# Inverse roots of the norms: from a power on GpSimd to Newton steps on VectorE, with shorter gaps between the steps of a chain

## The chip, the cores and the metric

The kernel runs on one core of a Trainium2 chip. The time is device microseconds of one execution, given as the median of several runs; a smaller number is better. A profile of one execution of the kernel before stands beside the times. In the profile PE is TensorE's matmuls and PEld its weight loads, DVE is VectorE, ACT is ScalarE, POOL is GpSimd and SP is SyncE, from which most DMAs are issued.

## The reference

Two transformer layers, each an attention part and a mixture of experts, are applied to 8 sequences of 256 tokens with 128 features. Each of the four parts takes a layer norm of its input and adds its result to the residual:

```python
def _layernorm(x, axis=-1, eps=1e-05):
    m = jnp.mean(x, axis=axis, keepdims=True)
    v = jnp.var(x, axis=axis, keepdims=True)
    return (x - m) / jnp.sqrt(v + eps)

x = x + _L0_attn_ref(_layernorm(x), ...)   # latent-projection attention, 16 heads, causal softmax
x = x + _L0_ffn_ref(_layernorm(x), ...)    # top 2 of 8 experts, gelu; the result is normed again
x = x + _L1_attn_ref(_layernorm(x), ...)   # RMS norm, linear attention in segments of 32
x = x + _L1_ffn_ref(_layernorm(x), ...)    # top 2 of 8 experts, relu
```

Layer 0's expert part ends in a norm of its own, `(out - mean) * rsqrt(var + 1e-5) * gamma + beta`. Layer 1's attention takes an RMS norm of the layer-normed input. In both expert parts a router picks two of eight experts for each token. All is in fp32.

## The kernel before, in words

The 2048 tokens are worked on as four blocks of 512 (`NBLK` = 4; a block is four tiles of 128 tokens). Layer 0's attention goes by rows, one row being one sequence, so two rows make a block and there are eight in all (`Row`, `attention0`). A row's norm is of two tiles (values 128x2), a block's of four (128x4).

After attention a block goes through the router (`route0` or `route1`: norm, logits, top 2), `dispatch` (each token gets slots, and POOL scatters the rows `hrows` to DRAM with 8 indirect DMAs), `experts` (15 tiles of slots, each with weights loaded by SP; ACT applies the function to the hidden layer at L510), `chosen` (POOL gathers the two results `yt` of each token with 8 indirect DMAs) and then `combine0` and `before1` (layer 0: weigh and norm the results, then norms, projections and gates for layer 1's attention) or `finish` (layer 1: add and store).

The order of the work is written out by hand. Steps are Python generators. `beside` runs the steps of attention, and after each of them `Lines.go` advances a clock of its own: PART0 is 2.0 units in 4 slots, PART1 is 1.5 units in 3 slots, so a slot is half a unit. In each slot at most one step of the line "chain" (routers, dispatches, gathers, combines) is put down, and experts by credit. A chain step is due again `APART` = 1.0 unit after it ran, or after what it yields:

```python
wait = next(steps, self)
if wait is not self:
    if line == "chain":
        queue.append((self.now + (wait or APART), steps, then))
```

What is put down in this way is ordered by a scheduler of the language into one list for each engine; `behind(...)` and `follow(...)` tie instructions to a place in it. Each engine then works through its list in order, and an instruction at the head of a list that waits for another engine holds up everything behind it.

There are 24 norms: eight of rows, four in `route0`, four in `combine0`, four in `before1` and four in `route1`. In 20 of them `rsqrt` (L272) adds the epsilon on DVE (L275), has POOL raise to the power -0.5 with the constant tile `mhalf` (L276), and DVE scales with the result (L295 in `layernorm`, L930 in `combine0`). In `before1` the layer norm and the RMS norm are made together: four small DVE instructions (L945 to L948), one power of 128x8 on POOL (L950), and the scaling at L955. In the routers and in the rows the scaling is put off by one step (`later[0]()`), after a gap of 1.5 units in the routers, as after the power in `combine0` and `before1`; a row's steps follow those of attention.

Of the kernel before, what the change touches and what calls it, by code (L numbers as in the profile page):

```python
# [36 lines left out]
ALU = mybir.AluOpType  # L37
# [3 lines left out]
P = 128  # L41
B, S, D = 8, 256, 128
NBLK = 4
NT = 4
# [34 lines left out]
def two_layers(  # L79
# [6 lines left out]
    nc = tc.nc  # L86
    cp = ctx.enter_context(tc.tile_pool(name="const", bufs=1))
    wk = ctx.enter_context(tc.tile_pool(name="work", bufs=2))
    sm = ctx.enter_context(tc.tile_pool(name="small", bufs=3))
# [8 lines left out]
    def tl(pool, shape, tag, dt=FP, bufs=None):  # L98
        kw = {} if bufs is None else {"bufs": bufs}
        return pool.tile(shape, dt, tag=tag, name=f"{tag}_{next(names)}", **kw)  # L100

    def bank():
        return tl(ps1, [P, 512], "mm")
# [16 lines left out]
    @contextmanager  # L120
    def behind(*engines):

        seen = reversed(nc.cur_bb.bb.instructions)
        want, found = set(engines), []
        for i in seen:
            if i.engine in want:
                want.remove(i.engine)
                found.append(i)
                if not want:
                    break  # L130
        with ExitStack() as stack:
            for i in found:
                stack.enter_context(tc.issue_after(i))
            yield
# [58 lines left out]

    ident = tl(cp, [P, P], "ident")
    make_identity(nc, ident)
    mhalf = tl(cp, [P, 2 * NT], "mhalf")
    nc.gpsimd.memset(mhalf, -0.5)
    wqkv = tl(cp, [P, QK + KVH * HD], "wqkv")
    identb = tl(cp, [P, P], "identb", BF)
    causb, within = tl(cp, [P, G, P], "causb", BF), tl(cp, [P, G, 32], "within", BF)  # L200
# [67 lines left out]

    def rsqrt(src, eps):

        n = src.shape[1]
        r = tl(sm, [P, NT], "rsqrt")[:, 0:n]
        nc.vector.tensor_scalar(r, src, eps, None, ALU.add)  # L275
        nc.gpsimd.tensor_tensor(r, r, mhalf[:, 0:n], ALU.pow)  # L276
        return r

    def moments(src):
        n = src.shape[1]  # L280
# [7 lines left out]
    def layernorm(src, y, parts=None):  # L288

        mv = moments(src)  # L290
        r = rsqrt(mv[:, :, 1], 1e-5)

        def scaled():
            for t in range(src.shape[1]):
                nc.vector.tensor_scalar(  # L295
                    y[:, t, :], src[:, t, :], mv[:, t, 0:1], r[:, t : t + 1],
                    ALU.subtract, ALU.mult,
                )

        if parts is None:  # L300
            scaled()
        else:
            parts.append(scaled)
        return y

    def transposed(src, tag, eng, bufs=2):

        n = src.shape[1]
        pt = bank()
        for t in range(n):  # L310
            nc.tensor.transpose(pt[:, t * P : (t + 1) * P], src[:, t, :], ident)
        y = tl(wk, [P, n * P], tag, bufs=bufs)
        (nc.scalar.copy if eng == "act" else nc.vector.tensor_copy)(y, pt[:, 0 : n * P])
        return y

    def per_tile(ap):

        return ap.unsqueeze(1).to_broadcast([P, NT, ap.shape[1]])

    def last(ap, n):  # L320

        return ap.unsqueeze(2).to_broadcast([P, ap.shape[1], n])

    def small(tag, shape=(P, NT, E)):
        return tl(sm, list(shape), tag)
# [32 lines left out]
    def logits(xT, gw):  # L358
        pg = bank()
        for t in range(NT):  # L360
            nc.tensor.matmul(
                pg[:, t * E : (t + 1) * E], lhsT=xT[:, t * P : (t + 1) * P], rhs=gw,
                start=True, stop=True,
            )
        return pg[:, 0 : NT * E].rearrange("p (t e) -> p t e", e=E)
# [202 lines left out]
    def gated_bias(gates, b2s):  # L568

        pg = bank()  # L570
        for t in range(NT):
            nc.tensor.transpose(pg[0:E, t * P : (t + 1) * P], gates[:, t, :], ident)
        gT = tl(wk, [E, BT], "qm")
        nc.scalar.copy(gT, pg[0:E, :])
        pb = bank()
        for t in range(NT):
            nc.tensor.matmul(
                pb[:, t * P : (t + 1) * P], lhsT=gT[:, t * P : (t + 1) * P], rhs=b2s,
                start=True, stop=True,
            )  # L580
        return pb.rearrange("p (t o) -> p t o", t=NT)
# [287 lines left out]
    def route0(x, half):  # L869
        later = []  # L870
        xn = layernorm(x, half.rows, later)
        yield 1.5 * APART
        later[0]()
        nc.gpsimd.tensor_tensor(x, x, per_tile(bet), ALU.add)
        yield
        with behind(PE):
            xT = transposed(xn, "xTf", "vec")
        yield
        lg = small("lg")
        with behind(PE):  # L880
            nc.vector.tensor_copy(lg, logits(xT, gw0))
            psh = bank().rearrange("p (t o) -> p t o", t=NT)
            for t in range(NT):
                nc.tensor.matmul(
                    psh[:, t, :], lhsT=xT[:, t * P : (t + 1) * P], rhs=shw, start=True, stop=True
                )
        half.acc = acc = tl(wk, [P, NT, D], "acc", bufs=NBLK)
        nc.vector.tensor_tensor(acc, psh, per_tile(shb), ALU.add)
        hots = half.hots
        m1, m2 = top2(lg, hots)  # L890
        yield 2 * APART
        yield from dispatch(half, b1s0)
        tot = small("tot", (P, NT))
        nc.vector.tensor_tensor(tot, m1, m2, ALU.add)
        nc.vector.reciprocal(tot, tot)
        gates = tl(wk, [P, 2, NT, E], "gates")
        for k, m in enumerate((m1, m2)):
            g = half.gates[:, k, :]
            nc.vector.tensor_tensor(g, m, tot, ALU.mult)
            nc.vector.tensor_tensor(gates[:, k], hots[:, k], last(g, E), ALU.mult)  # L900
        nc.vector.tensor_tensor(gates[:, 0], gates[:, 0], gates[:, 1], ALU.add)
        nc.scalar.activation(acc, acc, AF.Gelu)
        yield
        with behind(PE):
            nc.vector.scalar_tensor_tensor(
                acc, acc, 0.5, gated_bias(gates[:, 0], b2s0), ALU.mult, ALU.add
            )

    def combine0(x, half, yt):
        acc = half.acc  # L910
        with behind(DVE):
            for t in range(NT):
                for k in range(2):
                    nc.vector.scalar_tensor_tensor(
                        acc[:, t, :], yt[:, k, t, :], half.gates[:, k, t : t + 1],
                        acc[:, t, :], ALU.mult, ALU.add,
                    )
        yield

        with behind(DVE):  # L920
            mv = moments(acc)
            r = rsqrt(mv[:, :, 1], 1e-5)
            for t in range(NT):
                nc.vector.scalar_tensor_tensor(
                    acc[:, t, :], acc[:, t, :], mv[:, t, 0:1], gam, ALU.subtract, ALU.mult
                )
        yield 1.5 * APART
        with behind(DVE):
            for t in range(NT):
                nc.vector.scalar_tensor_tensor(  # L930
                    x[:, t, :], acc[:, t, :], r[:, t : t + 1], x[:, t, :], ALU.mult, ALU.add
                )
# [5 lines left out]
    def before1(o, x):  # L938
# [3 lines left out]
        with behind(DVE):  # L942
            mv = moments(x)
            v, rr = mv[:, :, 1], small("norms", (P, 2, NT))
            nc.vector.tensor_scalar(rr[:, 0], v, 1e-5, None, ALU.add)  # L945
            nc.vector.reciprocal(rr[:, 1], rr[:, 0])
            nc.vector.tensor_tensor(rr[:, 1], rr[:, 1], v, ALU.mult)
            nc.vector.tensor_scalar(rr[:, 1], rr[:, 1], 1e-6, None, ALU.add)  # L948
            rr = rr.rearrange("p a t -> p (a t)")
            nc.gpsimd.tensor_tensor(rr, rr, mhalf, ALU.pow)  # L950
        r = rr[:, NT:]
        yield 1.5 * APART
        with behind(DVE):
            for t in range(NT):
                nc.vector.tensor_scalar(  # L955
# [284 lines left out]
    def route1(x, half):  # L1240
        later = []
        xn = layernorm(x, half.rows, later)
        yield 1.5 * APART
        later[0]()
        yield
        with behind(PE):
            xT = transposed(xn, "xTf", "vec")
        yield
        lg, hots = small("lg"), half.hots
        with behind(PE):  # L1250
            nc.vector.tensor_tensor(lg, logits(xT, gw1), per_tile(gb1), ALU.add)
        top2(lg, hots)
        yield 2 * APART
        yield from dispatch(half, b1s1)
        gates = tl(wk, [P, NT, E], "gates")
        nc.vector.tensor_tensor(gates, hots[:, 0], hots[:, 1], ALU.add)
        yield
        with behind(PE):
            nc.vector.tensor_tensor(x, gated_bias(gates, b2s1), x, ALU.add)
# [46 lines left out]
    APART = 1.0  # L1306
# [163 lines left out]
```

## Time and profile before

| | |
|---|---|
| median of 3 runs | 710.58 us (708.97 to 712.07) |
| profiled execution | 705.73 us, span 704.0 us |
| granted TensorE clock, mean | 0.912 of full speed |
| busy: PE, DVE, ACT, POOL | 569.2, 406.4, 333.9, 190.0 us |
| the powers on POOL | 20 of 927 ns and 4 of 1807 ns |

Busy time is the sum of an engine's instructions. A group of instructions is shown as line, engine, operation, output and inputs with their shapes and count, then its busy time and the mean ns of one, then the engine's idle time just before them with what ended it. In the table of waits, each row names who waited, for whom, the total in us, how often, and the longest. In the timeline, each row has the start, the duration, and in brackets the idle time before it. In the page's second part a digit is the busy share in one of 40 equal slices of the span.

### The profile page before, as it was taken

To read this page: it belongs to the slowest core of one execution; us is meant where nothing else is said; L and a number is where in the kernel's file an instruction comes from. 1 tells how busy PE (TensorE), PEld (TensorE's weight loads), DVE (VectorE), ACT (ScalarE), POOL (GpSimd) and SP (SyncE) were. 2 spreads that over 40 slices of the span, in tenths; PEclk is the share of its full clock that TensorE was granted. 3 is DMA by queue.
4 is the path that set the end of the run, shared out by engine and by line. 5 is a ranking of instruction groups with operands and counts; after the bars stand their busy time and mean duration, and the time that the engine had idled before them with its cause. 6 is when DMAs were issued, how large, how long until landed. Compare 5 with 4: busy or idle time off the path is not lost. (4 is left out here: it accounts for less than half of the span.)

```text
span 704.0 us, 13677 instructions
## 1 busy us (share of the span) xinstructions
PE 569.2 (81%) x4830; PEld 427.4 (61%) x4846; DVE 406.4 (58%) x1193; ACT 333.9 (47%) x761; POOL 190.0 (27%) x223
## 2 busy tenths in 40 slices
PE   5577786998989788967899579979889898988570
PEld 3233353676646466536688467758867788987570
DVE  4765665536645566536687289787875877531201
ACT  2233342877858489842464224633444233443240
POOL 4201105001144210442113511434603340441204
PEclk9999988999899899997999779989998999999795
DMA  6800004453164414453345624546464658878662
GB/s 163 225 2 0 1 2 138 132 169 114 35 187 132 119 47 135 132 150 95 97 125 170 209 62 139 159 124 172 136 198 138 183 162 239 248 228 272 170 180 56
DMA packets 132100, 95.81 MB, mean 136 GB/s; under 512 B 8817, under 2 KB 114369, under 8 KB 132033
## 3 DMA queue, kind: packets, MB, share of 16 engines
q1 hardware_dynamic: 127520, 85.58, 41.7%
q0 software_dynamic: 4096, 8.40, 4.2%
q10 hardware_dynamic: 416, 0.96, 0.5%
q8 instruction: 39, 0.64, 0.4%
q14 instruction: 29, 0.23, 0.1%
HBM read 77.87 MB, written 17.04 MB: 135 GB/s over the span
## 5 line engine op out<-in xcount | busy, mean ns | idle before, releaser
L510 ACT ACTIVATE hT<-mm,bias 128x128 f32<-128x128 f32 x480 | 136.3, 371 | 136.3 <-PE mm L503 127.8
L503 PE MATMUL mm<-xrT,w 128*128 128x128 f32 x960 | 140.7, 295 | 23.9 <-DMA w<-in_w 10.4
L503 PEld LDWEIGHTS mm<-xrT,w 128*128 128x128 f32 x960 | 126.5, 206 | 41.4 <-DVE xrT L487 12.6
L515 PE MATMUL mm<-w,hT 128*128 128x128 f32 x960 | 137.4, 285 | 7.5 <-ACT hT L510 5.3
L515 PEld LDWEIGHTS mm<-w,hT 128*128 128x128 f32 x960 | 123.4, 198 | 17.7 <-ACT hT L510 13.7
L432 POOL DMA_INDIRECT xg<-hrows,slots x64 | 66.0, 1032 | 110.3 <-DVE slots L424 56.0
L559 POOL DMA_INDIRECT yt<-yg,slots x64 | 61.3, 958 | 110.3 <-issue 50.0
L727 ACT ACTIVATE at<-sc 128x1024 f32<-128x1024 f32 x48 | 48.8, 1023 | 56.3 <-PE sc L780 56.1
L780 PE MATMUL sc<-qm,kxT 32*128 32x512 f32 x192 | 54.9, 682 | 11.5 <-ACT at L727 4.6
L780 PE MATMUL sc<-km,qT 32*128 32x512 f32 x192 | 55.6, 701 | 4.2 <-DVE qx L688 2.3
L688 DVE TENSOR_REDUCE nmax<-sc 128x8 f32<-128x1024 f32 x32 | 38.9, 1220 | 24.9 <-PE sc L780 24.9
L276 POOL TENSOR_TENSOR rsqrt<-rsqrt,mhalf 128x4 f32<-128x4 f32 (+1 forms) x20 | 18.5, 927 | 122.7 <-DVE rsqrt L275 98.1
L523 DVE COPY ys<-mm 128x512 f32<-128x512 f32 (+1 forms) x32 | 20.8, 651 | 38.7 <-PE mm L515 38.5
L1120 DVE TENSOR_TENSOR at<-sc,consts 128x1024 f32<-128x1024 f32 x32 | 38.0, 1214 | 6.2 <-PE sc L1115 5.8
L510 ACT ACT_TABLE_LOAD x25 | 32.1, 1283 | 15.3 <-PE mm L503 15.0
L780 PEld LDWEIGHTS <-identb 32*32 32x32 bf16 (+1 forms) x320 | 7.6, 91 | 39.2 <-issue 37.3
L1058 POOL TENSOR_TENSOR vm<-va,consts 128x432 f32<-128x432 f32 x16 | 14.6, 932 | 59.2 <-ACT hT L510 19.7
L487 DVE COPY xrT<-mm 128x512 f32<-128x512 f32 (+1 forms) x32 | 20.8, 651 | 15.9 <-PE mm L486 15.8
L738 PE MATMUL mm<-at,vx 128*32 128x512 f32 x192 | 26.7, 630 | 4.1 <-ACT at L727 4.0
L780 PEld LDWEIGHTS sc<-qm,kxT 32*128 32x128 f32 x192 | 14.4, 191 | 25.0 <-issue 9.4
L1115 PE MATMUL sc<-pqm,kT 32*128 32x512 f32 x128 | 23.2, 800 | 6.9 <-DVE at L1120 4.9
L1139 ACT COPY rope<-mm 128x512 f32<-128x512 f32 x16 | 9.4, 588 | 40.3 <-PE mm L1133 40.3
(212 smaller groups left out, 935.6 us busy)
## 6 DMA issues: line engine op xcount, KB each, us to landing
w<-in_w SPq DMA_DIRECT2D x240, 256.0 KB, 3.4
xr<-xg SPq DMA_DIRECT2D x24, 256.0 KB, 3.2
yg<-ys SPq DMA_DIRECT2D x24, 256.0 KB, 4.5
xg<-zero SPq DMA_DIRECT2D x12, 256.0 KB, 2.9
xr<-xg SPq DMA_DIRECT2D x8, 192.0 KB, 5.2
yg<-ys SPq DMA_DIRECT2D x8, 192.0 KB, 4.1
x<-in_x SPq DMA_DIRECT2D x4, 256.0 KB
xg<-hrows,slots POOLq DMA_INDIRECT x64, 2.2
```

The lines of the kernel that those rows point to most:

```text
L432: i = nc.gpsimd.indirect_dma_start(out=xg_h[:, :], out_offset=bass.IndirectOffsetOnAxis(ap=half.slots[:, k, t : t + 1], axis=0), in_=half. ...
L487: nc.vector.tensor_copy(xrT[:, 0 : n * P], pt[:, 0 : n * P])
L503: nc.tensor.matmul(ph[:, c * P : (c + 1) * P], lhsT=w1s[:, c * P : (c + 1) * P], rhs=xrT[:, t * P : (t + 1) * P], start=True, stop=True,)
L510: nc.scalar.activation(hT[:, c, :], src, func, bias=bias)
L515: nc.tensor.matmul(po[:, t * D : (t + 1) * D], lhsT=hT[:, c, :], rhs=w2s[:, c, :], start=(c == 0), stop=(c == NC - 1),)
L559: nc.gpsimd.indirect_dma_start(out=yt[:, k, t, :], out_offset=None, in_=yg[half.h][:, :], in_offset=bass.IndirectOffsetOnAxis(ap=half.slot ...
L688: return nc.vector.tensor_reduce(nm[:, js[0] : js[0] + 2, :], sc.rearrange("p j (i k) -> p j i k", i=G), AX.X, ALU.max, negate=True,)
L727: return nc.scalar.activation(pT[:, js[0] : js[0] + 2, :], sc, AF.Exp)
L738: nc.tensor.matmul(self.po[32 * j : 32 * j + 32, :], lhsT=self.vx[:, kt, j, :], rhs=self.pT_of[s][:, j, :], start=(kt == 0), stop=(kt == qt),)
L780: done[n].append(nc.tensor.matmul(*args, **kw))
L1115: nc.tensor.matmul(sc[j].rearrange("p (i k) -> p i k", i=G), lhsT=pkT[rows, cols], rhs=pqm[rows, :, cols], start=True, stop=True,)
L1120: nc.vector.tensor_tensor(at[:, 2 * a : 2 * a + 2].rearrange("p j i k -> p (j i) k"), d.rearrange("p j (i k) -> p (j i) k", i=G), const("t ...
```

## The change

The inverse root is worked out on DVE. A first guess comes from the bits of the value: they are shifted right by one as an integer, negated, and a constant is added. Then three Newton steps of three instructions each are taken, so a root is 11 instructions on 128x2, 128x4 or 128x8 values, each of which reads what the one before wrote. POOL no longer takes part, and the constant tile `mhalf` goes. In `route0`, `combine0`, `before1` and `route1` the gap of 1.5 units behind the norm's statistics becomes the usual 1.0, which is two slots where it was three. The rows of layer 0's attention have no such gap.

```diff
-    mhalf = tl(cp, [P, 2 * NT], "mhalf")
-    nc.gpsimd.memset(mhalf, -0.5)
...
+    def root(v):
+
+        n = v.shape[1]
+        y, z = (tl(sm, [P, 2 * NT], k, bufs=4)[:, 0:n] for k in ("root", "step"))
+        yi = tl(sm, [P, 2 * NT], "rooti", I32)[:, 0:n]
+        nc.vector.tensor_scalar(yi, v.bitcast(I32), 1, None, ALU.logical_shift_right)
+        nc.vector.tensor_scalar(y.bitcast(I32), yi, -1.0, float(0x5F3759DF), ALU.mult, ALU.add)
+        for _ in range(3):
+            nc.vector.tensor_tensor(z, v, y, ALU.mult)
+            nc.vector.scalar_tensor_tensor(z, z, -0.5, y, ALU.mult, ALU.mult)
+            nc.vector.scalar_tensor_tensor(y, z, 1.5, y, ALU.add, ALU.mult)
+        return y
+
     def rsqrt(src, eps):
 
-        n = src.shape[1]
-        r = tl(sm, [P, NT], "rsqrt")[:, 0:n]
-        nc.vector.tensor_scalar(r, src, eps, None, ALU.add)
-        nc.gpsimd.tensor_tensor(r, r, mhalf[:, 0:n], ALU.pow)
-        return r
+        v = tl(sm, [P, NT], "rsqrt")[:, 0 : src.shape[1]]
+        nc.vector.tensor_scalar(v, src, eps, None, ALU.add)
+        return root(v)
...
     # route0, combine0, before1 and route1, once each
-        yield 1.5 * APART
+        yield
...
     # before1
-            rr = rr.rearrange("p a t -> p (a t)")
-            nc.gpsimd.tensor_tensor(rr, rr, mhalf, ALU.pow)
+            rr = root(rr.rearrange("p a t -> p (a t)"))
```

More of the change, by code (lines that the diff above doesn't have):

```diff
@@ L266, in values_of_zeros @@
             nc.gpsimd.memset(by_head(t)[:, :, :, HD], 1.0)
-    def rsqrt(src, eps):
-        n = src.shape[1]
-        r = tl(sm, [P, NT], "rsqrt")[:, 0:n]
-        nc.vector.tensor_scalar(r, src, eps, None, ALU.add)
-        nc.gpsimd.tensor_tensor(r, r, mhalf[:, 0:n], ALU.pow)
-        return r
+    I32 = mybir.dt.int32
+    def root(v):
[9 more added lines that the diff above has]
+        return y
+    def rsqrt(src, eps):
+        v = tl(sm, [P, NT], "rsqrt")[:, 0 : src.shape[1]]
+        nc.vector.tensor_scalar(v, src, eps, None, ALU.add)
+        return root(v)
     def moments(src):
@@ L926, in combine0 @@
                 )
-        yield 1.5 * APART
+        yield
         with behind(DVE):
@@ L948, in before1 @@
             nc.vector.tensor_scalar(rr[:, 1], rr[:, 1], 1e-6, None, ALU.add)
-            rr = rr.rearrange("p a t -> p (a t)")
-            nc.gpsimd.tensor_tensor(rr, rr, mhalf, ALU.pow)
+            rr = root(rr.rearrange("p a t -> p (a t)"))
         r = rr[:, NT:]
-        yield 1.5 * APART
+        yield
         with behind(DVE):
@@ L1242, in route1 @@
         xn = layernorm(x, half.rows, later)
-        yield 1.5 * APART
+        yield
         later[0]()
```

## The prediction

> **What bounds the kernel now.** I read the page first, then the groups by line (idle before each group), the table of waits, and the timeline where the waits are long.
>
> ```profile
> span 704.0 us, 13677 instructions
> PE 569.2 (81%) x4830; PEld 427.4 (61%) x4846; DVE 406.4 (58%) x1193; ACT 333.9 (47%) x761; POOL 190.0 (27%) x223
> DVE  4765665536645566536687289787875877531201
> ```
>
> TensorE (PE) is busy 81% of the span, and its order is fixed[...]. VectorE (DVE) has 58% on average, but in the middle of the second half single slices stand at 8 and 9 tenths. GpSimd (POOL) has time to spare; what matters there is its queue.
>
> ```profile
> L276 POOL TENSOR_TENSOR rsqrt<-rsqrt,mhalf 128x4 f32<-128x4 f32 (+1 forms) x20 | 18.5, 927 | 122.7 <-DVE rsqrt L275 98.1 <-DVE mv L285 24.4
> L950 POOL TENSOR_TENSOR norms<-norms,mhalf 128x8 f32<-128x8 f32 x4 | 7.2, 1807 | 27.6 <-DVE norms L948 16.7 <-DVE mv L285 10.9
> L295 DVE TENSOR_SCALAR hrows<-x,mv,rsqrt 128x128 f32<-128x128 f32 x32 | 9.1, 342 | 21.6 <-POOL rsqrt L276 21.6
> L295 DVE TENSOR_SCALAR xn<-x,mv,rsqrt 128x128 f32<-128x128 f32 x16 | 5.0, 340 | 14.1 <-POOL rsqrt L276 14.1
> L930 DVE SCALAR_TENSOR_TENSOR x<-acc,rsqrt,x 128x128 f32<-128x128 f32 x16 | 4.8, 346 | 3.8 <-POOL rsqrt L276 3.8
> L955 DVE TENSOR_SCALAR xl<-x,mv,norms 128x128 f32<-128x128 f32 x16 | 4.4, 340 | 2.5 <-POOL norms L950 2.5
> ```
>
> There are 24 norms (20 + 4). A power takes POOL 0.93 or 1.81 us, and DVE stands still for its result 21.6 + 14.1 + 3.8 + 2.5 = 42.0 us in all. Four of these waits are far longer than a power: 13.43, 6.79, 4.61 and 2.83 us, 27.7 together; in those the power stood on POOL's queue behind eight (the last: four) indirect DMAs of about 1.25 us. The other 14.3 us are about 0.8 a norm. What the long ones cost PE is in the waits and in the timeline around 404 us:
>
> ```profile
> PE mm L311 <- DVE xrT L487: 9.9, 1, 9.9
> PE mm L587 <- DVE on L760: 7.9, 3, 6.1
> ```
>
> ```profile
> 400.50 0.94 POOL L559 DMA_INDIRECT yt<-yg,slots  x1 [0.30 <-issue]
> 401.46 1.78 POOL L1058 TENSOR_TENSOR vm<-va,consts 128x432 f32<-128x432 f32 x2
> 403.19 1.05 POOL L276 TENSOR_TENSOR rsqrt<-rsqrt,mhalf 128x4 f32<-128x4 f32 x1
> ```
>
> ```profile
> 390.67 0.17 DVE L275 TENSOR_SCALAR rsqrt<-mv 128x4 f32<-128x4 f32 x1
> 404.27 1.11 DVE L295 TENSOR_SCALAR hrows<-x,mv,rsqrt 128x128 f32<-128x128 f32 x4 [13.43 <-POOL rsqrt L276]
> 408.16 2.18 DVE L914 SCALAR_TENSOR_TENSOR acc<-yt,hgates,acc 128x128 f32<-128x128 f32 x8
> ```
>
> PE lost 9.9 us in the 13.43 us stall, 6.1 (the longest of L587) in the 6.79, 1.3 in the 4.61 and nothing in the 2.83: 17.3 of 27.7.
>
> **The change, part by part.**
>
> *1. Price of a root on DVE.* Eleven instructions on 128x2 to 128x8, each reading the one before. The nearest rows are a chain of small DVE instructions in the router:
>
> ```profile
> 608.56 0.18 DVE L335 RECIPROCAL ssum<-ssum 128x4 f32<-128x4 f32 x1
> 608.77 0.19 DVE L336 TENSOR_TENSOR sm<-sm,ssum 128x32 f32<-128x32 f32 x1
> 609.00 0.19 DVE L346 TENSOR_REDUCE top<-sm 128x4 f32<-128x32 f32 x1
> ```
>
> So 0.21 to 0.23 us from start to start when each waits for the last; 0.21 for these smaller shapes, 2.3 us a root. The integer shift and the integer multiply-add have no row; between 0.15 (a plain 128x4 scalar op) and twice that each, I take the plain one; the upper end adds 24 x 2 x 0.15 = 7 us of DVE. An independent instruction starts only about 0.1 us after the one before, so a step with other work ahead of it adds some 0.1. In the built order of the changed kernel, 179 of the 240 steps inside roots follow their predecessor directly and 61 have something between. Added DVE time: (24 + 179) x 0.21 + 61 x 0.1 = 49 us against 42 us of stalls removed. For DVE as a whole it is nearly an exchange; the places decide.
>
> [...]
>
> *2. The start: +5.5.* In the changed order DVE does row 0's root, row 1's statistics, row 1's root, and only then the copy that PE waits for.
>
> ```profile
> 4.54 0.17 DVE L275 TENSOR_SCALAR rsqrt<-mv 128x2 f32<-128x2 f32 x1
> 5.43 0.27 DVE L213 COPY oT<-mm 64x128 f32<-64x128 f32 x1
> 5.75 0.79 PE L214 MATMUL mm<-wqb,oT 64*128 64x128 f32 x2 [1.12 <-DVE oT L213]
> ```
>
> The copy at 5.43 moves to 4.75 + 2.3 + 1.3 (statistics and two scalings, as now) + 2.3 + 0.3 = about 10.9. PE's chain to the first scores hangs on it and no other work covers it.
>
> *3. The long stalls: -13.* The power leaves POOL's queue, so the DMAs no longer stand ahead of it. At 404 us the next thing late is the gather itself: in the changed order the eight L914 (there L925) still stand ahead of the copy that the router's matmuls need, and the last gathered rows land at about 403, so that copy moves from 410.3 to some 404: -6 of PE's 9.9. At 119 us the operand that PE lacked now stands ahead of the scaling: -6. Of the other two, -1.
>
> *4. The other 18 norms: +11.* Their share of the added DVE time is 49 - 4.6 (start) - 7.5 (the four above) = 37; less 14.3 of old stalls, +22.5 us. On DVE's queue the score maxima (L688), the masks on scores (L1120) or the scalings stand directly behind, and PE waits for those. The long stalls gave PE 17.3/27.7 = 0.6 of their length; short ones meet more slack, so I take 0.5. Bounds: 0 (all in slack) and 0.8.
>
> *5. Activation tables: +2.5.* The build has 61 table loads where there were 57; a row gives 1.28 us each, 5.1 on ScalarE, between PE's hidden layer and its outputs. Half is taken, 0 and 5 are the ends.
>
> *6. The shorter gaps: 0.* Four steps a block come half a unit of the line's time earlier. The moved steps issue no DMA, but dispatch scatters, gathers, their stores and weight loads follow them in the queues of POOL and SP. In the built order PE is the same up to about 230 us; behind that the dispatch positions of the second layer stand 29 and 19 matmuls earlier, 36 later and unchanged, out of the program's 2774, and the last block's rows and all after it stand where they were. The gather in front of the 308 to 330 us gap (PE lost 7.8 there) stands as before. No direction follows; the ends are -8 and +10, one gap of that kind closed or opened. POOL's freed 26 us and the dropped memset cost nothing: POOL is 27% busy.
>
> Sum: 5.5 - 13 + 11 + 2.5 + 0 = +6 us. The profiled execution took 705.73 us (span 704.0 and 1.7 around it), so 711.7 in its terms; it stands 0.7% under the median, 710.58, and on that the forecast is 716.6.
>
> **The rivals.** *Faster: DVE's queue has slack where the roots go.* If the roots of step 4 fall into time in which DVE would wait for PE anyway (the table of waits has 24.9 us of L688's `nmax` waiting for scores), and the long stalls return all 17.3 us, the sum is 5.5 - 17.3 + 0.15 x 22.5 + 2.5 = -6: 704.6. It decides from the point where PE sees less than about a quarter of the short places. For it: DVE at 58%. Against it: slices at 8 and 9 tenths, and roots directly ahead of L688.
>
> *Slower by more: DVE becomes the bound between 420 and 570 us.* There it is busy 17 to 19 of 22 us. At a share of 0.8, with a new gap like that at 308 us: 5.5 - 13 + 18 + 2.5 + 3 = +16: 726.6. Against it: 21 us of stalls leave the same stretch.
>
> *No change.* Start, short places and long stalls cancel: 710.6.
>
> **How the numbers follow.** About 0.5%, 3.6 us, is what a measurement of this kernel can tell from no change. Likeliest case 0.56 (716.6, own range 711 to 723, from shares 0.3 to 0.75), faster 0.17, far slower 0.15, no change 0.12. With the likeliest case's lower edge counted as no change: faster 0.17, same 0.20, slower 0.63. The range 703 to 729 reaches into both outer cases.
>
> **What would show it.** Right: eleven roots' steps at 0.2 us pitch; L214 starting near 11 us; no DVE wait on POOL at a scaling; the 9.9 us PE wait shrunk to about 4 and the 6.1 gone; DVE busy up by some 40 us; more waits of PE for DVE on scores. Wrong: a pitch near 0.1, a start that moves by under 3 us, PE waits on L688 and L1120 unchanged, or one new gap of PE above 8 us, which would make step 6 the main term.

## The result and the profile after

| | before | after |
|---|---|---|
| median | 705.39 us (701.88 to 712.07, 20 runs) | 713.56 us (709.28 to 722.05, 20 runs) |
| profiled execution | 705.73 us, span 704.0 | 716.5 us, span 714.7 |
| granted TensorE clock, mean | 0.912 | 0.909 |

The changed kernel takes 1.0106 of the time before, with a 95% interval of 1.0074 to 1.0137. That is 7.5 us on the median before (5.2 to 9.7). The medians themselves stand 8.2 us apart, the two profiled executions 10.8. (Here and below, ratios and intervals are of the fast executions alone, those within 1.5% of their kernel's fastest, while medians are of all executions, so the two can differ.)

The page of the changed kernel, its span, the busy row, and VectorE in 40 slices:

```profile
span 714.7 us, 13929 instructions
PE 574.0 (80%) x4830; PEld 431.2 (60%) x4846; DVE 443.5 (62%) x1457; ACT 339.3 (47%) x765; POOL 165.1 (23%) x198
DVE  5665578446575755724687869786988787531111
```

DVE has 264 more instructions (24 roots of 11) and 37 us more of busy time. POOL has lost 25 us. PE is busy 4.8 us more for the same 4830 matmuls, and its idle time (span less busy time) has grown from 134.8 to 140.7 us, by 5.9. So in this pair of profiles the loss is of two kinds: longer waits of PE, and matmuls that took longer. The second kind differs from execution to execution (see the last section). The groups by line show what one step of a root costs (busy us in all and mean ns of one stand behind the bar):

```profile
L280 DVE SCALAR_TENSOR_TENSOR step<-step,root 128x4 f32<-128x4 f32 (+2 forms) x72 | 12.4, 173 | 1.6
L281 DVE SCALAR_TENSOR_TENSOR root<-step,root 128x4 f32<-128x4 f32 (+2 forms) x72 | 11.3, 158 | 1.6
L279 DVE TENSOR_TENSOR step<-rsqrt,root 128x4 f32<-128x4 f32 (+1 forms) x60 | 9.6, 160 | 1.4
```

Nothing on DVE waits for POOL at a scaling any more: L306, the scaling that was L295, had 21.6 + 14.1 us of it and now has no such wait. What PE waits for has changed its kind. The table of waits, PE's longest rows and those on scores (total us, times, longest):

```profile
PE mm L514 <- DVE xrT L498: 13.9, 7, 3.9
PE mm L322 <- DVE xl L965: 11.3, 4, 7.1
PE mm L763 <- DVE os L755: 7.6, 1, 7.6
PE sc L791 <- DVE qx L699: 6.8, 4, 2.7
PE mm L514 <- DMA w<-in_w: 6.6, 3, 3.8
PE mm L212 <- DMA x<-in_x: 6.6, 1, 6.6
...
PE mm L322 <- DVE hrows L306: 4.5, 2, 2.5
...
PE sc L791 <- DVE nmax L699: 4.3, 3, 1.8
...
PE sc L1125 <- DVE at L1130: 0.3, 1, 0.3
```

The waits on scores before (maxima at L688, masks at L1120):

```profile
PE sc L1115 <- DVE at L1120: 4.9, 2, 3.9
PE sc L780 <- DVE nmax L688: 4.8, 3, 2.1
...
PE sc L780 <- DVE qx L688: 4.5, 4, 2.3
```

The single 9.9 us wait and the 6.1 us wait of before are gone. In their place stand a 6.6 us wait in the first matmuls (put down to the load of `x`, though what came last is DVE's copy, as the next view shows), more waits for the copies of transposed rows (L498), and somewhat longer ones for the score maxima: L699 (before L688), 11.1 us in all where they were 9.3. The waits for the masks fell from 4.9 to 0.3.

The start, in DVE's timeline of the changed kernel:

```profile
4.32 0.17 DVE L287 TENSOR_SCALAR rsqrt<-mv 128x2 f32<-128x2 f32 x1
4.53 0.17 DVE L276 TENSOR_SCALAR rooti<-rsqrt 128x2 int32<-128x2 int32 x1
4.73 0.17 DVE L277 TENSOR_SCALAR root<-rooti 128x2 int32<-128x2 int32 x1
4.93 0.16 DVE L279 TENSOR_TENSOR step<-rsqrt,root 128x2 f32<-128x2 f32 x1
...
6.50 0.16 DVE L281 SCALAR_TENSOR_TENSOR root<-step,root 128x2 f32<-128x2 f32 x1
...
7.61 0.16 DVE L287 TENSOR_SCALAR rsqrt<-mv 128x2 f32<-128x2 f32 x1
...
10.70 0.27 DVE L211 COPY oT<-mm 64x128 f32<-64x128 f32 x1
```

and in PE's:

```profile
11.03 0.79 PE L212 MATMUL mm<-wqb,oT 64*128 64x128 f32 x2 [6.56 <-DMA x<-in_x]
```

A step follows the last after 0.20 us (ten steps in 1.97 us, from 4.53 to 6.50). Two roots stand ahead of the copy at 10.70, and the matmul that needs it starts at 11.03, where it started at 5.75 before: +5.3 us.

A row's norm in the middle of layer 0, DVE's timeline:

```profile
60.90 0.17 DVE L287 TENSOR_SCALAR rsqrt<-mv 128x2 f32<-128x2 f32 x1
61.11 0.17 DVE L276 TENSOR_SCALAR rooti<-rsqrt 128x2 int32<-128x2 int32 x1
...
63.28 0.60 DVE L306 TENSOR_SCALAR xn<-x,mv,root 128x128 f32<-128x128 f32 x2
63.80 1.22 DVE L699 TENSOR_REDUCE qx<-sc 128x8 f32<-128x1024 f32 x1
```

and PE's:

```profile
65.16 0.74 PE L791 MATMUL sc<-qm,kxT 32*128 32x512 f32 x2 [2.69 <-DVE qx L699]
```

The score maximum, 1.22 us of DVE, waits behind the root, and PE's next scores wait for that maximum: 2.69 us with nothing else to do. It is one of the places that the loss comes from; what it costs is measured below, in rows_on_pool.

The former 404 us stall, first PE and then DVE:

```profile
417.98 1.00 PE L322 MATMUL mm<-ident,hrows 128*128 128x128 f32 x4 [2.52 <-DVE hrows L306]
...
425.28 1.16 PE L514 MATMUL mm<-xrT,w 128*128 128x128 f32 x8 [2.21 <-DVE xTf L324]
```

```profile
417.22 0.35 DVE L925 SCALAR_TENSOR_TENSOR acc<-yt,hgates,acc 128x128 f32<-128x128 f32 x1 [4.20 <-DMA yt<-yg,slots]
417.49 1.11 DVE L306 TENSOR_SCALAR hrows<-x,mv,root 128x128 f32<-128x128 f32 x4
```

PE waits 2.5 + 2.2 us where it waited 9.9. DVE stood 4.20 us for gathered rows just ahead of the scaling: the power is no longer late, the gather is. In DVE's order two of the eight instructions that take gathered rows (L925) stand ahead of the scaling, so the scaling still comes 10.2 us after its add of epsilon (407.34 to 417.49), where the power made it 13.6.

The former 119 us stall, PE's timeline, now later in the same chain:

```profile
137.05 1.08 PE L497 MATMUL mm<-ident,xr 128*128 128x128 f32 x4 [4.25 <-DMA xr<-xg]
```

PE's 6.1 us wait is gone, and shortly after that place PE waits 4.25 us for the load of scattered rows.

### The profile page after: what moved, and what is told of

It reads as the page before. It is cut to its first block, busy times and chain, and to the rows that moved or that the text cites. A ratio compares the mean times of both kernels' runs of the same rounds, so it can differ in the third digit from the quotient of the medians.

```text
span 714.7 us, 13929 instructions
## 1 busy us (share of the span) xinstructions
PE 574.0 (80%) x4830; PEld 431.2 (60%) x4846; DVE 443.5 (62%) x1457; ACT 339.3 (47%) x765; POOL 165.1 (23%) x198
## 5 line engine op out<-in xcount | busy, mean ns | idle before, releaser
L514 PE MATMUL mm<-xrT,w 128*128 128x128 f32 x960 | 144.5, 301 | 26.4 <-DVE xrT L498 13.9
L514 PEld LDWEIGHTS mm<-xrT,w 128*128 128x128 f32 x960 | 130.9, 213 | 41.1 <-DVE xrT L498 16.7
L791 PE MATMUL sc<-qm,kxT 32*128 32x512 f32 x192 | 57.0, 706 | 12.0 <-DVE qx L699 5.1
L791 PE MATMUL sc<-km,qT 32*128 32x512 f32 x192 | 58.1, 731 | 3.6 <-DVE nmax L699 1.8
L699 DVE TENSOR_REDUCE nmax<-sc 128x8 f32<-128x1024 f32 x32 | 38.9, 1221 | 22.9 <-PE sc L791 22.9
L498 DVE COPY xrT<-mm 128x512 f32<-128x512 f32 (+1 forms) x32 | 20.8, 652 | 23.6 <-PE mm L497 23.6
L699 DVE TENSOR_REDUCE qx<-sc 128x8 f32<-128x1024 f32 x16 | 19.6, 1223 | 13.5 <-PE sc L791 13.3
L633 POOL TENSOR_TENSOR x<-x,bout 128x256 f32<-128x256 f32 x8 | 5.8, 723 | 80.8 <-DVE xn L306 47.3
```

The source lines that it names most:

```text
L498: nc.vector.tensor_copy(xrT[:, 0 : n * P], pt[:, 0 : n * P])
L514: nc.tensor.matmul(ph[:, c * P : (c + 1) * P], lhsT=w1s[:, c * P : (c + 1) * P], rhs=xrT[:, t * P : (t + 1) * P], start=True, stop=True,)
L699: return nc.vector.tensor_reduce(nm[:, js[0] : js[0] + 2, :], sc.rearrange("p j (i k) -> p j i k", i=G), AX.X, ALU.max, negate=True,)
L791: done[n].append(nc.tensor.matmul(*args, **kw))
```

## The experiments

The twelve kernels ran in three groups, each on another chip. The first and third chip granted TensorE a mean clock of 0.86 to 0.88 in the profiles (the kernel before takes 754 to 755 us there), the second one near 0.91 (707 us). So every ratio below is to the kernel before in the same group, and ratios of different groups are set side by side only with that in mind. Each ratio is of five rounds, with its 95% interval.

Norms are told apart as "rows" (the eight norms of layer 0's attention, on 128x2 values) and "blocks" (the other sixteen).

### Group 1: roots and gaps apart (before: 754.34 us)

**roots_only**, the roots without the shorter gaps:

```diff
     # route0, combine0, before1 and route1 of the changed kernel
-        yield
+        yield 1.5 * APART
```

> The roots on VectorE, the gaps of 1.5 units kept: TensorE's order is that of the kernel before but for a few rows. Theory (the roots' own time on VectorE, at places where TensorE waits for it): all of the loss is here, +8 us against the kernel before (ratio 1.011, 1.007 to 1.015), with the first scores 5.3 us later as in the changed kernel. Rival 1 (the moved chain steps, that is the new order, cost the time): ratio 1.000 to 1.004. Rival 2 (the two parts are worth as much each): 1.005.

Measured: 762.76 us, 1.0122 [1.0070, 1.0173]. The roots alone carry the whole loss, within this interval.

**gaps_only**, the shorter gaps with the powers still on POOL:

```diff
     # route0, combine0, before1 and route1 of the kernel before
-        yield 1.5 * APART
+        yield
```

> The power on GpSimd as before, the four gaps at 1.0 unit: TensorE's order is nearly that of the changed kernel. Theory (the roots' own time): no change beyond 2 us either way, ratio 0.997 to 1.003. Rival 1 (the order): +6 to +8 us, ratio 1.009 to 1.011. Rival 2 (half each): 1.005.

Measured: 752.06 us, 0.9937 [0.9903, 0.9970]; ACT has 765 instructions, as in the changed kernel, where the kernel before has 761. So the four extra activation-table loads (61 after, 57 before, 1.28 us each) come with the gaps, not with the roots, and the gaps cost nothing in spite of them. DVE still waits for the powers (before, the same two rows had 21.6 us with 13.4 as the longest, and 14.1 with 6.8):

```profile
DVE hrows L295 <- POOL rsqrt L276: 16.4, 6, 10.0
...
DVE xn L295 <- POOL rsqrt L276: 13.9, 7, 6.8
```

What exactly the gaps gain was not found, and its size is not secured: the medians of all executions, 752.06 and 754.34 us, stand 0.3% apart. With the roots in place the gaps returned about 0.1% (1.0122 against 1.0106, on different chips and inside both intervals). Whether the two parts add is not resolved.

**start_on_pool**, the changed kernel with the norms of the first two rows by a power on POOL:

```diff
     def rsqrt(src, eps):
...
         nc.vector.tensor_scalar(v, src, eps, None, ALU.add)
-        return root(v)
+        norms_made.append(src.shape[1])
+        if len(norms_made) <= 2:
+            nc.gpsimd.tensor_tensor(v, v, mhalf[:, 0 : src.shape[1]], ALU.pow)
+            return v
+        return root(v)
```

> The changed kernel, but the norms of the first two rows are raised to the power on GpSimd; everything else is as in the changed kernel. Theory (a delay at the start is passed on to the end): 5.3 us less than the changed kernel, so +3 us against the kernel before, ratio 1.004. Rival (later waits for loads and gathers swallow the early delay): no less than the changed kernel, ratio 1.011.

Measured: 762.81 us, 1.0101 [1.0041, 1.0160]. At 124 us it lags the kernel before by 7.8 us, where roots_only lags by 13.2, so the 5.4 us of the start are there; at the end the interval cannot tell it from the changed kernel, and the theory's 1.004 lies just outside it. That the start's loss reaches the end is not shown by this run (rows_on_pool, below, does show it in PE's waits).

**six_steps**, six Newton steps for three:

```diff
-        for _ in range(3):
+        for _ in range(6):
```

> The changed kernel with six Newton steps where it has three: each root has 9 more instructions at 0.197 us, 1.8 us more on VectorE in each of the 24 norms, 42 us of VectorE time in all. Theory (TensorE sees the whole root at the start and about half of it elsewhere): 3.6 us more at the start and 20 elsewhere, about +32 us against the kernel before, ratio 1.045. Rival (VectorE has slack at all places but the start): +12 us, ratio 1.017.

Measured: 800.48 us, 1.0626 [1.0574, 1.0678]. 24 x 9 more instructions at 0.197 us are 42.6 us of DVE; against the changed kernel's 1.0112 (after_again, on another chip) the time grew by 0.051 of 754 us, about 39 us. Against start_on_pool, on the same chip, PE's idle time in the profile grew by 29 us (152.2 to 181.5). The waits of PE show where:

```profile
PE mm L322 <- DVE xl L965: 29.8, 4, 11.9
PE mm L514 <- DVE xrT L498: 11.9, 5, 4.5
PE sc L791 <- DVE nmax L699: 10.8, 4, 6.4
```

The wait for the four block scalings of L965 is 29.8 us, against 11.3 in the changed kernel (13.5 in start_on_pool, on the same chip) and 8.6 in gaps_only, which has the short gaps and the powers. So the roots of 2.2 us add 3 to 5 us there, and the further 1.8 us in each of the four add 16 or more.

### Group 2: which norms (before: 706.96 us)

**after_again** is the changed kernel once more, with no edit, to have it on the same chip as the next three.

> The changed kernel once more, on the chip on which its variants run, as their mark. Ratio to the kernel before 1.011 (1.007 to 1.014). If the parts add up, the roots alone (1.0122) and the gaps alone (0.9937) would give 1.006; if they do not, 1.011.

Measured: 715.54 us, 1.0112 [1.0049, 1.0175].

**two_steps**, the same line with `range(2)`; the root is less exact, its last step left out:

```diff
-        for _ in range(3):
+        for _ in range(2):
```

> The changed kernel with two Newton steps instead of three (the roots are less exact): 3 instructions fewer in each of 24 roots, 14.2 us of VectorE time at 0.197 us each. Theory A (VectorE time added inside a root shows nearly in full, as six steps did: 39 us more than the changed kernel for 42 us): 13 us less than the changed kernel, ratio to before about 0.993. Theory B (half of it shows, as the prediction took): 7 us less, ratio 1.001.

Measured: 705.57 us, 0.9959 [0.9932, 0.9987]. 72 instructions, 14.2 us of DVE, are worth 0.0153 x 707 = 10.8 us: a share of 0.76. The interval of after_again alone is 4.5 us to each side, so this run by itself does not exclude the 0.5 that the prediction took for most norms. PE's idle time in the two profiles, 140.2 us in after_again and 128.7 here, agrees with the larger share (its profiled execution took 711.1 us, more than the median), and so do the 39 of 42.6 us of the longer root. Together they say that DVE's root is on PE's path for most of its length, all norms taken together.

**rows_on_pool**, the changed kernel with the power on POOL in the eight rows' norms; the sixteen block norms keep their roots:

```diff
+        if src.shape[1] == 2:
+            nc.gpsimd.tensor_tensor(v, v, mhalf[:, 0 : src.shape[1]], ALU.pow)
+            return v
         return root(v)
```

> The changed kernel, but the eight norms of rows raise to the power on GpSimd; the 16 norms of blocks keep the root on VectorE. TensorE's order is that of the changed kernel. Theory A (the full time shows): the start gains 5.3 us, four rows 1.4 us each, and the two long waits of rows come back with 6.7 us net: 4 us less than the changed kernel, ratio to before 1.005. Theory B (only the start and the long waits show): 1.4 us more than the changed kernel, ratio 1.013.

Measured: 701.41 us, 0.9919 [0.9892, 0.9947]. Every theory missed, and by much: 0.0193, or 13.6 us, less than the changed kernel, with the order of PE's matmuls the same. The place shown above, in DVE's timeline of this kernel:

```profile
56.59 0.17 DVE L294 TENSOR_SCALAR rsqrt<-mv 128x2 f32<-128x2 f32 x1
57.58 0.60 DVE L317 TENSOR_SCALAR xn<-x,mv,rsqrt 128x128 f32<-128x128 f32 x2 [0.82 <-POOL rsqrt L297]
58.10 1.22 DVE L710 TENSOR_REDUCE qx<-sc 128x8 f32<-128x1024 f32 x1
```

and PE's:

```profile
59.46 0.70 PE L802 MATMUL sc<-qm,kxT 32*128 32x512 f32 x2 [1.29 <-DVE qx L710]
```

From the add of epsilon to the maximum it takes 1.51 us (56.59 to 58.10) where the root makes it 2.90 (60.90 to 63.80): 1.4 us, and PE's wait shows just that, 2.69 against 1.29. All waits for the maxima together are 7.2 us here and 11.4 in after_again. As the order of the matmuls is the same, the lead over after_again at any matmul splits into idle time and busy time of PE up to it (us, at the time of after_again):

| at | 25 | 75 | 125 | 200 | 225 | 300 | 400 | 500 | 600 |
|---|---|---|---|---|---|---|---|---|---|
| lead | 5.5 | 7.8 | 8.7 | 8.6 | 5.3 | 11.9 | 12.0 | 11.9 | 9.7 |
| of it less waiting | 5.5 | 7.7 | 8.7 | 9.0 | 8.4 | 9.2 | 9.5 | 9.5 | 9.0 |
| of it shorter matmuls | 0.0 | 0.1 | 0.0 | -0.5 | -3.0 | 2.6 | 2.5 | 2.4 | 0.7 |

So the rows' roots cost PE some 9 us of waits, 5.5 at the start and 3.5 at the other six, and these are kept: they stand between 8.4 and 9.5 at all later points of the table, and over the whole span they are 12.5 (140.2 against 127.7). What comes and goes is the matmuls' own time. The profiled executions differ by 10.1 us at the end, the medians by 14.1; the interval on 13.6 is near 5 us to each side.

**long_stalls_only**: short gaps, powers on POOL in 21 norms, and the root on DVE only in the three norms whose power had stood longest behind POOL's DMAs (the sixth and the eighth row's, and the first block's router norm of layer 1):

```diff
+        if len(norms_made) - 1 not in (6, 9, 14):
+            nc.gpsimd.tensor_tensor(v, v, mhalf[:, 0 : src.shape[1]], ALU.pow)
+            return v
         return root(v)
...
     # before1
-            rr = root(rr.rearrange("p a t -> p (a t)"))
+            rr = rr.rearrange("p a t -> p (a t)")
+            nc.gpsimd.tensor_tensor(rr, rr, mhalf, ALU.pow)
```

> The short gaps, the power on GpSimd in 21 norms, and the root on VectorE only in the three where the power stood behind eight indirect DMAs (waits of 6.8, 4.3 and 10.0 us in the profile of the gaps alone). TensorE's order is exactly that of the gaps alone. Theory A (a stall of VectorE shows nearly in full): 21.1 us of waits against 6.6 us of roots, 14 us less than the gaps alone, ratio to before 0.975. Theory B (behind the stall the next instruction waits for the gathered rows anyway): 2 to 6 us less than the gaps alone, ratio 0.985 to 0.991.

Measured: 691.63 us, 0.9767 [0.9715, 0.9820]. It beats both kernels, by 15 us the one before. It is 9.8 us faster than rows_on_pool on the same chip too, though it has roots in two rows: PE's idle time is 119.6 us, against 127.7 there, and most of that difference arises between 325 and 420 us, where block norms stand. The scaling of the last block's router in layer 0 comes 1.3 us after its add of epsilon here and 4.8 us after it in rows_on_pool. So some block roots cost time as well.

### Group 3: the parts of that gain (before: 755.3 us)

**gaps_again** is gaps_only once more.

> The gaps alone once more, beside the others on one chip: ratio to before 0.994 (0.990 to 0.997). If the first result was that chip's slower clock, 1.000.

Measured: 754.66 us, 0.9919 [0.9879, 0.9959]. By the ratio the gain stands; by the medians of all executions, 754.66 and 755.3 us, it is 0.1%. So a gain of some tenths of a percent is likely, and its size is not secured.

**rows_roots**: short gaps, the roots in the eight rows' norms, and powers on POOL in all sixteen block norms. The condition of the switch is `src.shape[1] != 2`, and `before1` keeps its power.

> The short gaps, the root on VectorE in the eight norms of rows and the power on GpSimd in the 16 of blocks: the complement of the run with the rows on GpSimd. Theory A (the parts add: the rows' roots cost the difference between the changed kernel and the run with rows on GpSimd, 0.0193): ratio to before 0.9937 + 0.0193 = 1.013. Theory B (a delay early in the run is swallowed by later waits as long as the blocks' norms are quick): ratio under 1.003.

Measured: 762.79 us, 1.0104 [1.0075, 1.0132]. Against gaps_again the rows' eight roots cost 0.0185 of the time, 14 us, on this chip too, with the blocks left alone (8 us by the medians of all executions). Against the kernel before they are as much as the whole loss.

**one_root**: short gaps, and one root only, in the first block's router norm of layer 1 (condition `len(norms_made) - 1 != 14`).

> The short gaps, the root on VectorE in one norm only, that of the first router of layer 1 (the wait of 10.0 us behind eight gathers in the profile of the gaps alone); 23 norms raise to the power on GpSimd. TensorE's order is that of the gaps alone. Theory A (as the times of equal events in the three-root run read: the row's wait at 119 us returns nothing, since the load of the scattered rows is late next, and that at 200 us 2.3 us): 2 to 3 us more than with three roots, ratio to before 0.980. Theory B (each stall counts in full): 6.7 us more than with three roots, ratio 0.986.

Measured: 750.88 us, 0.9933 [0.9902, 0.9964]. Missed: it is not to be told from gaps_again. The trace shows that the root did not free the scaling. Its ninth instruction ends at 419.24 us, and the tenth stands in DVE's order behind a copy that waits for PE:

```profile
419.08 0.16 DVE L281 TENSOR_TENSOR step<-rsqrt,root 128x4 f32<-128x4 f32 x1
423.95 0.69 DVE L509 COPY xrT<-mm 128x512 f32<-128x512 f32 x1 [4.71 <-PE mm L525]
424.56 0.15 DVE L282 SCALAR_TENSOR_TENSOR step<-step,root 128x4 f32<-128x4 f32 x1
...
425.23 1.11 DVE L317 TENSOR_SCALAR hrows<-x,mv,root 128x128 f32<-128x128 f32 x4
```

The scaling comes 10.0 us after its add of epsilon (415.22), where the power in gaps_again makes it 9.7. PE's waits at this place are some 3 us shorter than in gaps_again, not 9.9. (The profiled execution took 758.6 us, more than the median.) In long_stalls_only this norm's scaling also comes 8.9 us after its add of epsilon, and in the next run 9.3.

**long_old_gaps**: long_stalls_only with the old gaps of 1.5 units, so that PE's order is that of the kernel before.

> The kernel before with the gaps of 1.5 units, and the root on VectorE only in the three norms behind eight indirect DMAs (waits of 6.79, 4.61 and 13.43 us in the profile of before). TensorE's order is exactly that of the kernel before. Theory A (the gaps are worth their 0.006 by themselves): ratio to before 0.983. Theory B (the short gaps gained because the long wait is 10.0 us in them instead of 13.43, which is gone here): as good as with three roots and short gaps, ratio 0.977.

Measured: 751.89 us, 0.9930 [0.9897, 0.9963]. Missed, too: three roots return 0.7% where 1.7% was the least that was expected.

Put together, with short gaps throughout:

| rows' norms | blocks' norms | ratio, chips near 0.88 | ratio, chips near 0.91 |
|---|---|---|---|
| POOL | POOL | 0.9937, 0.9919 | not run |
| POOL | DVE | not run | 0.9919 |
| DVE | POOL | 1.0104 | not run |
| DVE | DVE | not run | 1.0106, 1.0112 |

The step from POOL to DVE in the rows is +0.0185 in the left column and +0.019 in the right, each within one chip. The blocks' net, near nothing, is read only across columns, and is therefore an inference: on one chip it was not measured. It is a balance: some of these roots cost (long_stalls_only), and the one at the 404 us stall returns a part.

What stays open is the size of the selective version. Its 0.9767 was measured on the faster-clocked chip alone; on the slower ones one_root and long_old_gaps gave 0.993 each. A run of long_stalls_only on a slower-clocked chip would tell, and was not made.

## Why the prediction was right, and where it was not

The forecast was +6 us; +8.2 was measured by the medians, and slower was the sign given most of the chance. (The forecast of 716.6 us stood on 710.58, the median of three executions; with 20 the kernel before takes 705.39.) PE's idle time, which the sum was about, grew by 5.9 us in the profile after and by 5.4 in after_again, on another chip. But the sum comes out by two errors that cancel. Against the terms of the prediction, in PE's waits between the profiles before and after, read just ahead of each place and just behind it:

| | predicted | waits of PE |
|---|---|---|
| start | +5.5 | +5.3 |
| long stalls | -13 | -5.5, from three of the four |
| other norms, table loads, gaps | +13.5 | +6.1, the rest |
| sum | +6 | +5.9 |

That the two errors, some 7.5 us each, are of one size is luck. The longer matmuls, +4.8 in this pair and +3.1 in after_again, were no term of the sum. Of the signs that were named for it, one did not come: with the masks, PE's waits for DVE on scores fell, from 14.2 to 11.4 us.

**Step 1, the price of a root: right.** 0.197 us from step to step against 0.21 taken, 2.2 us a root against 2.3. The integer shift and multiply-add took 0.17 us each, as the addition of epsilon ahead of them did. In the rows, where one operation on POOL becomes eleven on DVE, the kernel is 13.6 us faster with the power on POOL. For norms whose power stood behind POOL's DMAs long_stalls_only points the other way, with the size left open above.

**Step 2, the start: right in place and size**, +5.3 us against +5.5.

**Step 3, the long stalls: the direction right, the size off by more than half.** -13 was the term; PE's waits returned 5.5. At 404 us they fall from 12.3 us over those of before to 8.2, -4.1 where -6 was written. (The lag of the matmuls themselves falls by more, from 17.0 to 11.3 us, as they also ran faster there.) The step named what would be late next, the gather, but held its landing at about 403 us, while the profile after has gathers issued from 410 on, because they wait for a store that itself came late, the first of them by 18 us (410.04, before 391.70):

```profile
410.04 0.97 POOL L570 DMA_INDIRECT yt<-yg,slots  x1 [16.39 <-DMA yg<-ys]
```

At 119 us -6 was written and nothing came back (waits 7.0 us over before ahead of the place, 6.9 behind it): "the operand that PE lacked now stands ahead of the scaling" was true, and the next thing late, the load of scattered rows at 137.05 with its 4.25 us, was not looked for. At 200 us the waits fell by 1.3, all that PE had lost there, as written (-1 for the two smaller stalls).

**Step 4, the other norms: one share for places that differ.** One share of 0.5 for all 18 norms gave +11; with table loads and gaps +13.5 was forecast, and +6.1 is what is left. The runs part the norms only in part. Of the rows, the six behind the start cost 3.5 us of PE's waits net of what rows_on_pool keeps of the two long stalls. Their roots stand directly ahead of a maximum that PE waits for, 1.4 us later than with the power at the place shown. By the whole times of rows_on_pool and after_again the eight rows cost 13.6 us; what this has beyond the waits is in part the length of matmuls and in part within the interval. The block roots are near nothing net, read across chips, but not all of them are in slack.

**Step 5, the table loads: the cause was wrong.** They belong to the gaps (gaps_only has them with no root), and the net of both is no loss without the roots.

**Step 6, the gaps: 0 was inside its ends.** Alone they return 0.6 to 0.8% by the ratios, some 5 us, and 0.1 to 0.3% by the medians; with the roots in place about 1 us, unresolved.

The error of step 3, some 7.5 us too much given back, was covered by the 13.5 us of steps 4 to 6, which were too much by as much. The runs do not part that second error between norms, table loads and gaps. Of the rivals, the faster one needed the rows' roots in slack, which they are not. The far slower one needed DVE as the bound between 420 and 570 us. PE's waits there are over those of before by 8.2 us at 423 and by 7.6 at 601, so it is refuted for three Newton steps.

## What to carry to other kernels

A chain of small dependent instructions costs its step from start to start, here 0.2 us, times its length, and whether that is paid depends on what stands directly behind it on that engine's queue: price a moved operation place by place, not with one share for all. Look also at what stands between its steps: a chain that was moved to escape one wait can be held by another in its new queue (in one_root 4.71 us of DVE's idle time, behind a copy that waits for PE). An operation that stands behind DMAs (here eight, issued 1.25 us apart) and one whose engine is free are different cases: try the two kinds of place apart. When a stall is removed, look for the next operand that comes late, and remember the gather that waits for a store: here the first one came 18 us later than before (410.04 against 391.70), after POOL had stood 16.39 us for that store.

## What the runs showed of the hardware

The mean granted clock differed between chips, 0.91 on one and 0.88 on two, and the kernel before took 707 us on the first and 754 to 755 on the others. From 126 to 178 us the profile of gaps_only, from a slower-clocked chip, is still within 0.15 us of that of before; the difference arises later.

Inside one execution the granted clock falls to 0.5 for 3 to 14 us at a time (16 to 20 at the very end), at places that move from one execution to the next: in the profile after it is 0.5 at 32 to 42 us, where before has 1.0, and in that of before at 65 to 69. Of the 8.4 us that the profile after lags at 39 to 53 us of before, 4.6 are busy time of PE for the same matmuls; rows_on_pool, which has no root at the start, lags by 4.0 there and has 6.0 of it. Two single profiles compared by position carry such differences, so it pays to compare idle time as well.

One step of a root on 128x2 values took 0.63 us where its neighbours take 0.16:

```profile
8.99 0.63 DVE L280 SCALAR_TENSOR_TENSOR step<-step,root 128x2 f32<-128x2 f32 x1
```

No wait stands with it. It is no accident of one execution: after_again has 0.67 us at 8.59, roots_only 0.71 at 8.88, and both have 0.72 in another row's root, near 175 us. Its cause is open.
